# Two stages of normalised residual blocks: another order of the 26 products of a group, and set places in it for the next unit's preparation

## The chip, the cores and the metric

The kernel runs on one core of a Trainium2 chip. The core has a matrix engine (PE, whose weight loads the profile lists as PEld), three engines that work on vectors (DVE, ACT and POOL), and a queue on SyncE (SP) from which this kernel issues its DMAs, in order. The metric is the time of one execution on the device in microseconds (us); a version is given by the median of its runs.

## The reference

The input x is 2 × 2048 × 1024 in float32. Two blocks with a modulation computed from c follow each other: attention over the channels of a normalised x (a score matrix per position), and then, with nearly all of the work, a feed-forward network with 1024 inputs, 2752 hidden values and a SiLU gate:

```python
    mod = (_silu(L0_c) @ L0_wmod).reshape(L0_c.shape[0], 6, 1, -1)
    ...
    h = _layernorm(x, axis=-1) * (1 + ca) + sa
    x = x + ga * _L0_attn_ref(h)
    h = _layernorm(x, axis=-1) * (1 + cb) + sb
    x = x + gb * _L0_ffn_ref(h, L0_ffn_W_gate, L0_ffn_W_up, L0_ffn_W_down)
```

```python
        up = jnp.einsum('td,fd->tf', xf, W_up)
        gate = jax.nn.silu(jnp.einsum('td,fd->tf', xf, W_gate))
        h = gate * up
        y = jnp.einsum('tf,df->td', h, W_down)
```

## The kernel before

**Units.** The tokens are cut into 8 units of 256 tokens in each of the two batch entries. A unit has a *gate and up* part (hidden values, left in H) and a *down* part. All large products are made from float16 pairs: an operand is split into a high and a low half (`split`: L241 on ACT makes the high half, L245 on DVE the low one), and three of the four partial products are summed in float32.

**Gate and up.** Two tiles of 128 hidden values with their gate and up weights are a pair; there are 10 pairs of f-tiles, an extra tile (the 21st, number NP) and a left-over of 64 values. A pair can be computed *as is* (`gu_as_is`, 4 weight tiles with 48 matmuls of 128x256 each), or two pairs together as a *group* (`gu_group`): a fast matrix multiplication with 26 products where the plain way has 32. A product is 12 matmuls (L1110); the left operands (sums of weight blocks) are made once by `build` (after `G_LEFT`) and kept in DRAM as dq, the right operands (sums of blocks of the normalised x) once per unit by `right_gu` (after `G_RIGHT`). `G_STEPS` lists the 26 products in order: right operand, accumulator (six, on the PSUM tags X, Y, Z with two banks each), whether the accumulator is started anew, and the reads after it. A read is a copy to SBUF on ACT (`c`, L1114), an addition or subtraction on DVE (`+`, `-`, `r`, L1124), a SiLU on ACT (`s`, L1116) or the product of gate and up on DVE (`h`, L1120). `G_ROWS` says which block of the weights and tokens is which.

Unit 0 computes all pairs plainly and unit 1 as is. Units 2 to 7 run 3, 4, 5, 5, 5 and 5 groups, then what pairs are not in groups. Units 1, 2 and 3 build the left operands (3, 1 and 1 groups) beside their as-is pairs, with 2, 2 and 4 steps of `build` at each tick. After the pairs come the maximum for the scale of H (`close_scale`, L1156; it ends in L211, sA), tile NP as is, the right operand of down's first step (`right_dn(0)`, three L241 and three L245), and the left-over (`gu_left_over`, 48 matmuls at L1135 into pl; L1142 and L1143 on ACT and L1145 on DVE read pl).

**Down.** Seven products of a fast 2 × 2 scheme (`DN_STEPS`), 120 matmuls each (L1266, accumulators dX, dY, dZ); `right_dn(si + 1)` is issued in step si; then the left-over's share (L1294, pB), the results and their stores (L1303).

**Preparation of the next unit.** `prep(u + 1)` is a generator with 43 pieces: loads of x (L793) and of the statistics, 8 pieces that apply the first normalisation, 16 that add the attention's result, the mean (on POOL, L812), 8 that form and square the deviations (L831, L836, L837), the variance, its reciprocal root (L229 on ACT, L232 to L235 on DVE) and 8 that scale and shift (each with two L847 on DVE and two L849 on ACT). A part is run by `tick` during gate and up:

```python
                if u == 1 or taken % 4 == 0:
                    run_gen(side)
```

The rest runs in down, five pieces in each of its first three steps and what is left in the fourth. From the fourth step on, and beside pB, `right_gu` makes the right operands of the next unit.

**Weights.** `Feed` (L581) loads the weight tiles from DRAM in the order of use: a tile of a group holds two products (512 KB); four tiles are ahead, in a pool of 5 buffers, which one holds until its last matmul is done.

**Order.** In unit 0 the order of the instructions is as written. From unit 1 on a scheduler orders the instructions of each engine, so the text above gives only the order in which they are handed to it; `tick` ties its pieces behind the latest reads of DVE and ACT.

Of the kernel before, what the change touches and what calls it, by code (L numbers as in the profile page):

```python
# [45 lines left out]

G_STEPS = (
    (2, 4, True, (('c', 0),)),
    (10, 2, True, (('c', 1),)),
    (12, 3, True, (('c', 2),)),  # L50
    (17, 4, False, (('+', 1, 1),)),
    (3, 3, False, (('c', 3),)),
    (25, 1, True, (('+', 3, 3),)),
    (6, 4, False, (('c', 4),)),
    (0, 1, False, (('+', 2, 2),)),
    (8, 3, False, (('-', 1, 1), ('-', 4, 5),)),
    (16, 4, False, ()),
    (9, 0, True, (('-', 1, 1), ('s', 1),)),
    (7, 5, True, (('+', 4, 4),)),
    (20, 4, False, (('-', 3, 3), ('h', 3, 1, 0, 0),)),  # L60
    (1, 3, False, (('-', 4, 4),)),
    (14, 0, False, (('-', 0, 0),)),
    (21, 4, True, (('c', 1),)),
    (23, 5, False, (('-', 1, 3),)),
    (13, 3, False, (('-', 1, 1),)),
    (22, 1, False, (('+', 5, 5), ('+', 3, 3),)),
    (4, 0, True, (('-', 1, 1),)),
    (11, 4, True, (('+', 0, 0), ('-', 5, 5),)),
    (24, 2, False, (('+', 5, 5), ('s', 5),)),
    (15, 3, False, (('-', 0, 0), ('-', 3, 3), ('s', 0), ('s', 3), ('h', 1, 3, 1, 1),)),  # L70
    (5, 5, False, ()),
    (18, 0, False, (('-', 4, 4), ('h', 4, 5, 1, 0),)),
    (19, 5, False, (('-', 2, 2), ('h', 2, 0, 0, 1),)),
)

G_LEFT = (
    ('e', 13, 1, 1), ('e', 12, 4, 1), ('e', 17, 10, 1), ('o', 't', 12, '-', 0), ('e', 15, 't', 1),
    ('o', 0, 0, '+', 1), ('o', 12, 12, '-', 0), ('o', 't', 0, '-', 10), ('e', 2, 't', 1), ('o', 't', 12, '+', 9),
    ('e', 11, 't', 1), ('o', 't', 2, '-', 0), ('e', 21, 't', 1), ('o', 16, 10, '+', 11), ('e', 10, 16, -1),
    ('o', 16, 9, '-', 16), ('o', 10, 10, '+', 12), ('o', 't', 10, '-', 8), ('e', 14, 't', 1), ('o', 8, 0, '-', 8),  # L80
    ('o', 't', 8, '-', 9), ('e', 9, 't', 1), ('o', 9, 9, '-', 13), ('e', 24, 9, -1), ('o', 9, 9, '+', 15),
    ('o', 't', 9, '-', 11), ('e', 6, 't', -1), ('o', 0, 4, '+', 0), ('e', 3, 0, 1), ('o', 't', 0, '-', 16),
    ('e', 8, 't', -1), ('o', 't', 5, '+', 0), ('e', 16, 't', -1), ('o', 15, 15, '+', 16), ('o', 16, 1, '-', 16),
    ('e', 1, 16, 1), ('o', 13, 13, '-', 15), ('o', 15, 15, '+', 12), ('o', 't', 3, '+', 13), ('e', 18, 't', -1),
    ('o', 't', 13, '-', 7), ('e', 20, 't', -1), ('o', 't', 13, '-', 2), ('e', 7, 't', 1), ('o', 3, 3, '+', 2),
    ('o', 't', 3, '-', 16), ('e', 4, 't', -1), ('o', 7, 6, '+', 7), ('e', 25, 7, 1), ('o', 2, 2, '-', 14),
    ('e', 23, 2, -1), ('o', 6, 6, '+', 2), ('o', 't', 6, '-', 4), ('e', 5, 't', -1), ('o', 14, 14, '-', 7),
    ('o', 't', 15, '+', 14), ('e', 22, 't', 1), ('o', 14, 13, '-', 14), ('e', 0, 14, -1), ('o', 't', 5, '-', 14),
    ('e', 19, 't', -1),
# [1 line left out]
G_RIGHT = (  # L91
    ('e', 9, 0), ('e', 24, 1), ('e', 16, 2), ('e', 19, 3), ('e', 23, 4), ('e', 25, 5), ('e', 26, 6), ('e', 4, 7),
    ('o', 't', 7, '-', 4), ('e', 7, 't'), ('o', 't', 4, '-', 5), ('e', 21, 't'), ('o', 5, 5, '-', 7), ('e', 5, 5),
    ('o', 5, 1, '+', 5), ('e', 12, 5), ('o', 't', 1, '-', 0), ('e', 14, 't'), ('o', 8, 0, '-', 2), ('e', 8, 8),
    ('o', 't', 8, '-', 6), ('e', 10, 't'), ('o', 't', 8, '-', 5), ('e', 3, 't'), ('o', 5, 0, '-', 5), ('e', 2, 5),
    ('o', 't', 8, '-', 7), ('e', 1, 't'), ('o', 2, 6, '+', 2), ('o', 't', 6, '-', 7), ('e', 18, 't'),
    ('o', 6, 4, '-', 6), ('e', 6, 6), ('o', 't', 6, '+', 5), ('e', 17, 't'), ('o', 7, 3, '+', 7), ('e', 20, 7),
    ('o', 't', 4, '-', 7), ('e', 0, 't'), ('o', 't', 7, '-', 0), ('e', 11, 't'), ('o', 't', 2, '-', 7),
    ('e', 22, 't'), ('o', 't', 7, '-', 1), ('e', 15, 't'), ('o', 1, 1, '-', 3), ('o', 't', 1, '-', 8),
    ('e', 13, 't'),  # L100
)
G_OPERAND = (0, 1, 2, 3, 4, 5, 6, 7, 8, 9, 10, 11, 12, 13, 14, 15, 16, 17, 18, 19, 6, 5, 20, 21, 22, 23)
G_PLAIN = (9, 24, 16, 19, 23, 25, 26, 4)
G_ROWS = ((1, 1), (0, 1), (0, 0), (1, 0))

PARTS = ((0, 0), (0, 1), (1, 0))

# [2 lines left out]
def adaln_kernel(ctx, tc, x, xT, wgp, wg20, wgl, wd, wd20, wd21, wmod, cT, out, nunits=NU):  # L110
# [34 lines left out]
    def right_of(o):  # L145
        return homes[made.index(o)]
# [5 lines left out]
    def place(i):  # L152

        return mix[:, 3 * D + i * 2 * TU:3 * D + (i + 1) * 2 * TU]
# [62 lines left out]
    def sumsq(src, col):  # L217
        n = src.shape[-1] * (src.shape[-2] if src.ndim > 2 else 1)
        j = evp.tile([P, D], BF16, tag="junk", name="junk", bufs=1) if n <= D else mix[:, 4 * D:].bitcast(BF16)
        p = src.shape[0]  # L220
        jv = j[0:p, 0:n]
        if src.ndim > 2:
            jv = jv.rearrange("p (a b) -> p a b", a=src.shape[1])
        S.activation(jv, src, AF.Square, accum_out=col)  # L224
# [280 lines left out]
    def gu_src(p):  # L505
        return wgp[p] if p < NP else wg20
# [73 lines left out]
    class Feed:  # L580
# [16 lines left out]
        def take(self):  # L597
            w = self.w.pop(0)
            self.ahead()
            return w  # L600
# [17 lines left out]
    def build(groups):  # L618
# [13 lines left out]
        def load(q, i):  # L632
            pair, up = G_ROWS[i // 2]
            Q.dma_start(regions[i], gu_src(2 * q + pair)[:, 2 * up + i % 2])
# [103 lines left out]
    class LeftOver:  # L738

        r = hpf  # L740
# [350 lines left out]
    def run_gen(g):  # L1091
        return next(g, 0) != 0
# [4 lines left out]
    def gu_group(q, take, asq, tick):  # L1097

        inv = inv_q[:, q:q + 1]
        acc = [ps.tile([P, 2, TU], F32, tag="XYZ"[i % 3], name=f"p{i}") for i in range(6)]  # L1100
        e = [place(i).rearrange("p (f c) -> p f c", f=2) for i in range(5)]
        e.append(evp.tile([P, 2, TU], F32, tag="ev", name="e", bufs=3))
        for at, (r, a, first, reads) in enumerate(G_STEPS):
            if at % 2 == 0:
                w2 = take().rearrange("p (t h f k c) -> p t h f k c", t=2, h=2, f=2, k=2)
            w, right = w2[:, at % 2], right_of(G_OPERAND[r])
            for f in range(2):
                for k in range(2):
                    for j, (wa, ha) in enumerate(PARTS):
                        T.matmul(acc[a][:, f], w[:, wa, f, k], right[:, ha, k], start=first and f == 0 and k == 0 and j == 0,  # L1110
                                 stop=k == 1 and j == 2, skip_group_check=True)
            for x in reads:
                if x[0] == "c":
                    mark["act"] = S.copy(e[x[1]], acc[a])  # L1114
                elif x[0] == "s":
                    mark["act"] = S.activation(e[x[1]], e[x[1]], AF.Silu, scale=inv)  # L1116
                elif x[0] == "h":
                    _, u, s, pair, n = x
                    p = 2 * q + pair
                    mark["vec"] = V.scalar_tensor_tensor(H[:, 2 * p:2 * p + 2, n], e[u], inv, e[s], ALU.mult, ALU.mult)  # L1120
                else:
                    sign, src, dst = x
                    in0, in1 = (acc[a], e[src]) if sign == "r" else (e[src], acc[a])
                    mark["vec"] = V.tensor_tensor(e[dst], in0, in1, ALU.add if sign == "+" else ALU.subtract)  # L1124
            tick()
        for p in (2 * q, 2 * q + 1):
            sumsq(H[:, 2 * p:2 * p + 2].rearrange("p f n c -> p (f n c)"), asq[:, p:p + 1])

# [19 lines left out]
    def unit(u, side, nxt):  # L1148
# [33 lines left out]
        wd_last = prep_wd_last()  # L1182
        taken = 0

        def tick(*_):
            nonlocal taken
            taken += 1
            if "vec" not in mark:
                return

            with tc.issue_after(mark["vec"].ins), tc.issue_after(mark["act"].ins):
                if at_build is not None:
                    for _ in range(at_build[1]):
                        run_gen(at_build[0])
                if u == 1 or taken % 4 == 0:
                    run_gen(side)

        at_build = None
# [52 lines left out]
        for si, (a, i) in enumerate(DN_STEPS):  # L1251
# [7 lines left out]
            for mm in range(4):  # L1259
                h, j = mm // 2, mm % 2  # L1260
# [448 lines left out]
```

## Time and profile before

| | |
|---|---|
| median of 3 runs | 2580.16 us (2575.6 to 2580.39) |
| profiled execution | 2579.11 us, its span 2577.3 us, TensorE clock granted 0.993 |
| PE busy | 2502.1 us, 97% of the span |
| DVE, ACT, POOL busy | 1905.7, 1060.2 and 117.1 us |
| matmuls of groups (L1110) | 8424, 273 ns each, one started every 109 ns |
| weight tiles of groups (wg from dq) | 351, 512 KB, 4.2 us from issue to landing |

Busy times are what the engine's instructions cover; matmuls overlap each other, so that a matmul of 273 ns takes 109 ns of PE when the next is ready. "Idle before <- releaser" is the time in which the engine stood and what its next instruction waited for. The profiled execution's own time is 1.8 us over its span. The times of units, where pl's last matmul starts in gate and up, are 363.98, 698.36, 1010.58, 1311.08, 1602.90, 1892.65, 2182.87 and 2472.41 us from the start of the span.

### The profile page before, as it was taken

How to read it: one execution, taken by the hardware profiler on the slowest of the kernel's cores; microseconds unless marked ns; L12 is line 12 of the kernel's file. 1: busy time of each engine (PE TensorE's matmuls, PEld its weight loads, DVE VectorE, ACT ScalarE, POOL GpSimd, SP SyncE). 2: the span in 40 equal slices, each digit the busy share in tenths (PEclk: the TensorE clock that was granted, in tenths of full speed). 3: DMA queues.
4: the chain of work that ended last, by engine and by line, in shares of the span. 5: the costliest groups of instructions: out<-in, count | busy, mean ns of one | idle time of the engine just before them, and what ended most of it. 6: DMA issues, size and time to landing. Idle time of an engine off the chain costs nothing.

```text
span 2577.3 us, 50942 instructions
## 1 busy us (share of the span) xinstructions
PE 2502.1 (97%) x21399; PEld 2054.2 (80%) x21399; DVE 1905.7 (74%) x3275; ACT 1060.2 (41%) x1613; POOL 117.1 (5%) x68
## 2 busy tenths in 40 slices
PE   7899969999999999999999999999999999999999
PEld 2344438888888888888888888888888888888887
DVE  8778686488986676966898667966697767954473
ACT  7768764144641343523454224412353224412230
POOL 6210000000000000000000000000000000000000
PEclk9999989999999999999999999999999999999999
DMA  9988866688566665666766765666656755656654
GB/s 391 398 320 316 305 234 218 231 273 267 191 195 229 223 236 169 200 228 204 268 221 198 234 195 185 203 229 201 199 187 196 235 194 182 203 194 199 197 185 156
DMA packets 162325, 585.58 MB, mean 227 GB/s; under 512 B 17584, under 2 KB 17648, under 8 KB 162096
## 3 DMA queue, kind: packets, MB, share of 16 engines
q1 hardware_dynamic: 162096, 582.33, 66.6%
q8 instruction: 167, 2.74, 0.4%
q14 instruction: 62, 0.51, 0.1%
HBM read 490.48 MB, written 91.78 MB: 226 GB/s over the span
## 4 chain that ended last, share of the span: by engine, by line
PE 83%; DVE 6%; DMA 6%; ACT 2%; issue 2%; POOL 0%; SPq 0%; DVEq 0%; ACTq 0%; POOLq 0%
PE p L1110 31%; PE g L1077 14%; PE dY L1266 12%; PE dX L1266 8%; PE dZ L1266 8%; DMA wg<-dq 5%; PE g L1051 4%; PE pB L1294 3%; PE pl L1135 1%; DVE bst L362 1%; PE pm L277 1%; DVE hbt L245 1%; ACT wq L241 1%; DVE mix L245 0%; DMA H<-in_wgp_dram 0%
## 5 line engine op out<-in xcount | busy, mean ns | idle before, releaser
L1110 PEld LDWEIGHTS <-wg 128*128 128x128 f16 x8424 | 821.9, 98 | 124.3 <-DMA wg<-dq 23.1
L1266 PEld LDWEIGHTS <-wd 128*128 128x128 f16 x6720 | 659.4, 98 | 91.7 <-issue 13.8
L1110 PE MATMUL p<-hbt,wg 128*128 128x256 f16 x4536 | 533.6, 273 | 12.1 <-DMA wg<-dq 12.1
L1124 DVE TENSOR_TENSOR mix<-mix,p 128x512 f32<-128x512 f32 x486 | 324.8, 684 | 293.0 <-PE p L1110 214.9
L1110 PE MATMUL p<-rot,wg 128*128 128x256 f16 x3564 | 427.2, 273 | 3.2 <-DMA wg<-dq 3.2
L1077 PE MATMUL g<-hbt,wg 128*128 128x256 f16 x3744 | 411.2, 273 | 0.0
L1077 PEld LDWEIGHTS <-wg 128*128 128x128 f16 x3744 | 366.4, 98 | 43.0
L1266 PE MATMUL dY<-rot,wd 128*128 128x256 f16 x2880 | 318.6, 273 | 0.0
L241 ACT ACTIVATE rot<-H,sA 128x1024 f16<-128x1024 f32 x168 | 163.0, 1000 | 208.7 <-PE dY L1266 76.6
L1266 PE MATMUL dX<-rot,wd 128*128 128x256 f16 x1920 | 216.6, 275 | 12.7 <-issue 6.0
L1051 PE MATMUL g<-hbt,wq 128*128 128x512 f16 x1008 | 219.6, 379 | 8.4 <-DVE wq L245 3.6
L1114 ACT COPY mix<-p 128x512 f32<-128x512 f32 x162 | 92.1, 584 | 307.9 <-PE p L1110 307.0
L1266 PE MATMUL dZ<-rot,wd 128*128 128x256 f16 x1920 | 213.2, 273 | 0.0
L245 DVE SCALAR_TENSOR_TENSOR rot<-H,sA,rot 128x1024 f16<-128x1024 f32 x168 | 181.4, 1098 | 42.8 <-ACT rot L241 42.7
L1051 PEld LDWEIGHTS <-wq 128*128 128x128 f16 x1008 | 97.9, 98 | 131.5 <-issue 5.9
L224 ACT ACTIVATE junk<-H 128x1024 bf16<-128x1024 f32 (+1 forms) x102 | 101.1, 991 | 152.3 <-DVE H L1087 82.5
L1116 ACT ACTIVATE mix<-mix,inv_q 128x512 f32<-128x512 f32 x81 | 55.5, 716 | 139.6 <-DVE mix L1124 139.3
L1116 ACT ACTIVATE e<-e,inv_q 128x512 f32<-128x512 f32 x27 | 19.5, 722 | 176.3 <-DVE e L1124 176.3
L812 POOL PARTITION_ALL_REDUCE mean<-acc x6 | 19.4, 3234 | 1472.8 <-DVE acc L825 1147.0
L1120 DVE SCALAR_TENSOR_TENSOR H<-mix,inv_q 128x512 f32<-128x512 f32 x81 | 60.7, 750 | 19.7 <-ACT mix L1116 18.0
L1294 PE MATMUL pB<-mix 128*128 128x512 f16 x320 | 74.6, 379 | 0.0
L1247 DVE SCALAR_TENSOR_TENSOR big<-dY,cA,big 128x256 f32<-128x256 f32 x96 | 41.8, 476 | 43.0 <-PE dY L1266 43.0
(350 smaller groups left out, 2548.0 us busy)
## 6 DMA issues: line engine op xcount, KB each, us to landing
wg<-dq SPq DMA_DIRECT2D x351, 512.0 KB, 4.2
wd<-dwd SPq DMA_DIRECT2D x224, 640.0 KB, 4.0
dq<-mix SPq DMA_DIRECT2D x130, 256.0 KB, 3.3
wg<-dgu SPq DMA_DIRECT2D x64, 512.0 KB, 4.5
dgu<-wq SPq DMA_DIRECT2D x40, 512.0 KB, 7.2
dwd<-hbt SPq DMA_DIRECT2D x28, 640.0 KB, 3.4
out_dram<-big SPq DMA_DIRECT2D x30, 512.0 KB, 3.5
big<-in_xT_dram SPq DMA_DIRECT2D x28, 512.0 KB, 5.8
```

Source lines behind the costliest of these rows:

```text
L224: S.activation(jv, src, AF.Square, accum_out=col)
L241: mark["hi"] = S.activation(dst_hi, src, AF.Copy, scale=s)
L245: return V.scalar_tensor_tensor(dst_lo, src, s, dst_hi, ALU.mult, ALU.subtract)
L1051: T.matmul(pt[m, f].rearrange("p n c -> p (n c)"), w[:, wa, f, k], hb0[:, ha, 4 * kh + k], start=kh == 0 and k == 0 and j == 0, stop=kh == ...
L1077: T.matmul(pt[m, f][:, n], w[:, wa, f, k], plain_of(2 * kh + k // 2, n)[:, ha, k % 2], start=kh == 0 and k == 0 and j == 0 and n == 0, sto ...
L1110: T.matmul(acc[a][:, f], w[:, wa, f, k], right[:, ha, k], start=first and f == 0 and k == 0 and j == 0, stop=k == 1 and j == 2, skip_group ...
L1114: mark["act"] = S.copy(e[x[1]], acc[a])
L1116: mark["act"] = S.activation(e[x[1]], e[x[1]], AF.Silu, scale=inv)
L1120: mark["vec"] = V.scalar_tensor_tensor(H[:, 2 * p:2 * p + 2, n], e[u], inv, e[s], ALU.mult, ALU.mult)
L1124: mark["vec"] = V.tensor_tensor(e[dst], in0, in1, ALU.add if sign == "+" else ALU.subtract)
L1266: T.matmul(acc[a, h][:, j], w[:, k // 5, wa, k % 5], rot16[:, si % 2, ha, k], start=(a, h) not in seen, stop=k == KH - 1 and jj == 2, skip ...
L1294: T.matmul(pB, wt[:, k, wa, m, :], hp[:, k, ha, :], start=i == 0, stop=i == len(LAST) - 1)
```

## The change

The 26 products of a group come in another order and use other accumulators. The products, their number, and the number of DVE reads (22, and 4 products of gate and up) stay; the copies of accumulators to SBUF on ACT go from 6 to 8 for a group, and one read has its operands exchanged (`r`). The signs of some left operands change with it (`G_LEFT`), the right operands are made in another order (`G_RIGHT`), and the blocks get other places (`G_ROWS`).

`tick` now gets the place of the product in the group. In a group a piece of the preparation is run after the products 3, 7, 12, 17, 18, 22 and 25 (counted from 0; `G_PIECES`), where it was each fourth tick. At ticks of as-is tiles it is run each time in units 2 and later (each fourth time before), and in unit 1 at three ticks of four (each tick before). Counted over gate and up, this is 30 pieces where there were 41 in unit 1, 41 for 24 in unit 2, 40 for 29 in unit 3 and 39 for 33 in units 4 to 6; unit 7 prepares nothing.

```diff
--- before.py
+++ after.py
@@ -46,44 +46,44 @@
 
 G_STEPS = (
     (2, 4, True, (('c', 0),)),
-    (10, 2, True, (('c', 1),)),
-    (12, 3, True, (('c', 2),)),
-    (17, 4, False, (('+', 1, 1),)),
-    (3, 3, False, (('c', 3),)),
-    (25, 1, True, (('+', 3, 3),)),
-    (6, 4, False, (('c', 4),)),
-    (0, 1, False, (('+', 2, 2),)),
-    (8, 3, False, (('-', 1, 1), ('-', 4, 5),)),
+    (12, 2, True, (('c', 1),)),
+    (7, 3, True, (('c', 2),)),
+    (9, 5, True, (('c', 3),)),
+    (3, 2, False, (('c', 4),)),
+    (17, 4, False, (('+', 3, 3),)),
+    (25, 0, True, (('+', 4, 4),)),
+    (10, 1, True, (('+', 3, 3),)),
+    (6, 4, False, (('c', 5), ('+', 2, 2),)),
+    (14, 5, False, (('+', 0, 0),)),
+    (8, 2, False, (('-', 3, 3), ('-', 5, 5), ('s', 3),)),
+    (0, 0, False, (('+', 1, 1),)),
     (16, 4, False, ()),
-    (9, 0, True, (('-', 1, 1), ('s', 1),)),
-    (7, 5, True, (('+', 4, 4),)),
-    (20, 4, False, (('-', 3, 3), ('h', 3, 1, 0, 0),)),
-    (1, 3, False, (('-', 4, 4),)),
-    (14, 0, False, (('-', 0, 0),)),
-    (21, 4, True, (('c', 1),)),
-    (23, 5, False, (('-', 1, 3),)),
-    (13, 3, False, (('-', 1, 1),)),
-    (22, 1, False, (('+', 5, 5), ('+', 3, 3),)),
-    (4, 0, True, (('-', 1, 1),)),
-    (11, 4, True, (('+', 0, 0), ('-', 5, 5),)),
-    (24, 2, False, (('+', 5, 5), ('s', 5),)),
-    (15, 3, False, (('-', 0, 0), ('-', 3, 3), ('s', 0), ('s', 3), ('h', 1, 3, 1, 1),)),
-    (5, 5, False, ()),
-    (18, 0, False, (('-', 4, 4), ('h', 4, 5, 1, 0),)),
-    (19, 5, False, (('-', 2, 2), ('h', 2, 0, 0, 1),)),
+    (11, 5, True, (('+', 0, 0), ('-', 5, 5),)),
+    (20, 4, False, (('-', 4, 4), ('h', 4, 3, 1, 0),)),
+    (1, 2, False, (('-', 2, 2),)),
+    (24, 1, False, (('+', 5, 5),)),
+    (4, 5, True, (('c', 3),)),
+    (23, 3, False, (('c', 4),)),
+    (13, 2, False, (('-', 3, 3),)),
+    (18, 5, False, (('+', 2, 2), ('s', 2),)),
+    (21, 1, True, (('-', 3, 3), ('+', 4, 4), ('s', 3),)),
+    (5, 3, False, ()),
+    (15, 2, False, (('-', 0, 0), ('+', 4, 4), ('s', 0),)),
+    (19, 3, False, (('-', 1, 1), ('h', 1, 0, 1, 1),)),
+    (22, 0, False, (('+', 5, 5), ('r', 4, 4), ('h', 5, 2, 0, 0), ('h', 4, 3, 0, 1),)),
 )
 
 G_LEFT = (
...
-    ('e', 11, 't', 1), ('o', 't', 2, '-', 0), ('e', 21, 't', 1), ('o', 16, 10, '+', 11), ('e', 10, 16, -1),
+    ('e', 11, 't', 1), ('o', 't', 2, '-', 0), ('e', 21, 't', -1), ('o', 16, 10, '+', 11), ('e', 10, 16, -1),
...
-G_ROWS = ((1, 1), (0, 1), (0, 0), (1, 0))
+G_ROWS = ((0, 0), (1, 1), (1, 0), (0, 1))
+G_PIECES = (3, 7, 12, 17, 18, 22, 25)
 
 PARTS = ((0, 0), (0, 1), (1, 0))
 
@@ -1122,7 +1123,7 @@
                     sign, src, dst = x
                     in0, in1 = (acc[a], e[src]) if sign == "r" else (e[src], acc[a])
                     mark["vec"] = V.tensor_tensor(e[dst], in0, in1, ALU.add if sign == "+" else ALU.subtract)
-            tick()
+            tick(at)
         for p in (2 * q, 2 * q + 1):
             sumsq(H[:, 2 * p:2 * p + 2].rearrange("p f n c -> p (f n c)"), asq[:, p:p + 1])
 
@@ -1182,7 +1183,7 @@
         wd_last = prep_wd_last()
         taken = 0
 
-        def tick(*_):
+        def tick(at=None):
             nonlocal taken
             taken += 1
             if "vec" not in mark:
@@ -1192,7 +1193,7 @@
                 if at_build is not None:
                     for _ in range(at_build[1]):
                         run_gen(at_build[0])
-                if u == 1 or taken % 4 == 0:
+                if at in G_PIECES or at is None and (u > 1 or taken % 4):
                     run_gen(side)
 
         at_build = None
```

## The prediction

> **What bounds the kernel now.** I read the page first, then the waits of PE, the chain of waits inside one unit, and the timeline at the end of two units.
>
> ```profile
> PE 2502.1 (97%) x21399; PEld 2054.2 (80%) x21399; DVE 1905.7 (74%) x3275; ACT 1060.2 (41%) x1613; POOL 117.1 (5%) x68
> ```
>
> PE is busy for 97% of the span, and the change leaves its 21399 matmuls as many as they are. So the only stock to win from is the time in which PE stands, and the only way to lose is to make it stand elsewhere. The waits of PE (total us, times, longest):
>
> ```profile
> PE p L1110 <- DMA wg<-dq: 15.3, 28, 2.1
> PE dX L1266 <- issue: 6.0, 1, 6.0
> PE dX L1266 <- ACT rot L241: 4.5, 1, 4.5
> PE dX L1266 <- ACT up L1143: 1.5, 1, 1.5
> ```
>
> No wait of a group's products is on DVE or ACT; all 28 are on the weight tiles. The 6.0 lies in unit 0, which the change leaves alone; the 4.5 ends unit 1's gate and up, the 1.5 unit 2's. In the matmul rows, starts follow each other by 109 ns, and counted against that L1110 loses 21.0 us in 29 places. Three are at the start of a unit (0.72 at 818.5, 1.03 at 1124.6, 2.30 at 1423.4, together 4.05); the other 16.95 are inside groups: one before the fifth product of nearly every group, and a second, up to 1.56, in five groups. The chain of waits in unit 4's gate and up (start, us, what):
>
> ```profile
> 1418.27 7.53 DMA wg<-dq
> ...
> 1450.94 4.14 DMA wg<-dq
> ...
> 1485.47 4.27 DMA wg<-dq
> ```
>
> A tile lands some 4.2 us after its issue, the issue waits for a free buffer of the five, and products wait for the landing. The timeline of unit 1's end (start, us, engine, line, operation; in brackets the idle time before):
>
> ```profile
> 700.53 0.15 DVE L211 TENSOR_SCALAR sA<-p2c 128x1 int32<-128x1 int32 x1
> 700.57 0.68 ACT L1142 ACTIVATE mix<-pl,inv_f 64x512 f32<-64x512 f32 x1
> 701.26 0.68 ACT L1143 ACTIVATE up<-pl,inv_f 64x512 f32<-64x512 f32 x1
> 701.97 2.80 ACT L241 ACTIVATE rot<-H,sA 128x1024 f16<-128x1024 f32 x3
> 703.16 2.21 DVE L245 SCALAR_TENSOR_TENSOR rot<-H,sA,rot 128x1024 f16<-128x1024 f32 x2 [0.49 <-ACT rot L241]
> 703.17 0.58 PE L1266 MATMUL dX<-rot,wd 128*128 128x256 f16 x2 [4.54 <-ACT rot L241]
> 704.49 7.72 PE L1266 MATMUL dX<-rot,wd 128*128 128x256 f16 x51 [0.74 <-DVE rot L245]
> ```
>
> The left-over's last matmul started at 698.36. sA is late, then the work of the left-over (L1142, L1143) stands ahead of L241 on ACT. The first dX follows the start of L241 by 1.20, the third by 2.52. The first 20 matmuls after the pause also run at 213 ns. In all 7.8 us are lost. Unit 4 shows the good order:
>
> ```profile
> 1595.83 2.80 ACT L241 ACTIVATE rot<-H,sA 128x1024 f16<-128x1024 f32 x3 [2.12 <-DVE sA L211]
> ...
> 1605.10 0.68 ACT L1142 ACTIVATE mix<-pl,inv_f 64x512 f32<-64x512 f32 x1
> 1605.80 0.68 ACT L1143 ACTIVATE up<-pl,inv_f 64x512 f32<-64x512 f32 x1
> ```
>
> L241 is 7 us ahead of the left-over's last matmul (1602.90), and down begins at once (1603.01).
>
> **The change part by part.** (1) *Order of products, inside groups.* After unit 0 a scheduler orders every engine, so I read the order in which each kernel issues. In before it interleaves: products of one tile stand up to 8.3 products' time apart, that tile holds its buffer, and from the release of a buffer to the first need of the tile loaded into it there pass 3.93 us for 22 tiles and 1.31 for 5. Against a landing of 4.2 that makes the waits seen. In after nearly every tile (323 of 351) is done in two products of 1.31; the shortest time from release to need is 5.0, mostly some 10. So −16.95. The 54 added copies (L1114, 8 for 6 a group, 584 ns) give ACT 31.5 us more work; it is 41% busy, its last PSUM reader of a group still ends before the accumulator is wanted, and DVE has the same 22 reads and 4 products a group. Cost 0; without that cover each late read would cost up to its own 0.6 to 0.7 us in 27 groups, 16 to 18 in all. G_LEFT's signs and G_RIGHT's order change no count; the operands wanted first are made some 15 us ahead.
>
> (2) *Unit starts.* SP's queue is in order. In units 2 to 6 the third load of xT, which waits for an out store to land (3.5), now stands ahead of the fourth store, so the fifth tile's issue comes 0.3 to 0.4 later; but the new order needs that tile one product, 1.31, later. Of 4.05 I expect 0 to 2 to stay (most likely 1, in unit 4): −3.
>
> (3) *A quarter less preparation in unit 1* (30 pieces for 41). DVE and ACT reach the scale earlier; L241 now stands ahead of L1142 and L1143. sA falls at about pl's last matmul, so the first dX comes some 1.3 after, the third 1.3 later: 2.0 to 3.2 lost in place of 7.8, no 213 ns. −5.3 (−4.7 to −5.8). The eleven pieces go to down. There four L232 (3.3) now stand ahead of the third part of step 1's operand (L245); by the sum of the rows between it is still done 1.8 before its matmul, so 0, and up to 2 if the rows run longer.
>
> (4) *Unit 2.* dX's bank is no longer the left-over's, and the right operand is early: −1.6.
>
> (5) *The end of the preparation, units 4 to 6.* Before, 33 of 43 pieces came ahead of down; now 39, so r2 (L232 to L235) and nearly all scalings (L847 on DVE, L849 on ACT) fall between the last group and down. By the orders, DVE does four L232 (905 ns, 3.3 together), L233 to L235 and 13 L847 ahead of the maximum that makes sA, so sA comes 15.3 us after the last group against 15.62 for pl's last matmul. On ACT, 16 L849, L1142 and L1143 now stand ahead of L241. L1142 starts 0.3 after pl's last matmul; then 0.70, one L849 of 0.42, 0.69 and L241's first 1.20: dX starts 3.3 after pl, its third matmul another 1.3 behind. Less the 109 ns a start and the two matmuls, that is 4.3 a unit, 12.9 in all. What this wait stops is the whole of down. The clock may fall on top: 4.82 idle did it (20 × 104 ns = 2.1), 2.30 at 1423.4 did not; a wait of 3.2 lies between, nearer 2.30, but 1.2 follows soon. I take half of 0 to 6.3: +3.
>
> ```profile
> L849 ACT ACTIVATE big<-big,sbs 128x256 f32<-128x256 f32 x96 | 41.4, 496 | 3.9 <-DVE big L847 3.9
> L847 DVE SCALAR_TENSOR_TENSOR big<-big,b1s,r 128x256 f32<-128x256 f32 x96 | 38.9, 475 | 0.0
> ```
>
> The Trainium skill, TensorE: Matmul & The Clock Gate, Part 1, puts the gate at an idle window of about 3.4 us: by it the pause of unit 1 cools the array and the one of 2.30 does not, as the rows have it, and one of 3.2 would not either. By that page the sum would be 3.0 lower than mine.
>
> (6) *Unit 3.* There DVE also builds left operands, four a tick, and has no idle time: summing its instructions between two reads of gate gives 20.06 and the trace 19.99. Eleven more pieces make it 11 us later: sA at 62.2 to 62.9 after the last group (before: 50), pl's last matmul at 57.8, the first dX at 64.1, the third 1.3 on. 7.4, and 1.9 for the clock after so long a pause: +9.3 (7 to 12). If the scheduler's neighbours hide some of the scalings it is less, if they queue up more.
>
> (7) *Down of units 2 to 6* loses some preparation; PE had no wait there, so 0. Unit 7 prepares nothing: 0.
>
> Sum: −16.95 − 3 − 5.3 − 1.6 + 12.9 + 3 + 9.3 = −1.7. Against the profiled execution's 2579.1 (span 2577.3 and 1.8 around it) that is 2577.4. It stood 1.1 under the median of the runs, whose three lie within 4.8; I leave that in the range, and take 2577.
>
> **Rivals.** *A, the gain stays whole.* Pauses (5) and (6) are short because ACT's and DVE's orders let L241 slip through earlier, or the executed row times are shorter than my sums: −27 with 3 to 14 back, 2555 to 2566. For it: the gains rest on slack that is counted (5.0 against 4.2), the losses on instructions' places. Against it: places on ACT are fixed, and the left-over's end comes first there.
>
> *B, slower: the clock falls in units 3 to 6 each time, and unit 3's DVE falls further behind.* Three times 6.4, unit 3 at 12 to 14, against −26.9: +4 to +8, and with a unit start that keeps its 4 us up to +10: 2584 to 2589. It decides from an idle time of about 3 us that already halves the clock, and an sA of unit 3 later than 66.
>
> *C, the waits for weights only move.* If the order of issue lets the release slip (SP holds stores of dq and loads of xT ahead of wg), half of the 17 stays: +7, 2582 to 2588. For it: SP was what held unit 4's start for 7.53. Against it: in groups its idle is the rule.
>
> *D, a group's accumulators make PE wait* for L1114 or L1124: 27 × 0.3 = 8, 2580 to 2587. Against it: no such wait in before with DVE at 74%.
>
> **How the numbers follow.** The forecast's case 0.52, A 0.22, B 0.12, C 0.08, D 0.06. The forecast's own range is 2570 to 2584 by (2), the half of the clock and unit 3. The overall one leaves out the lower part of A and the upper part of B: 2560 to 2587. A measurement of this kernel can tell about 0.2%, 5.2 us, from no change: faster is under 2575.0, slower over 2585.3. All of A and a third of the forecast's case are faster: 0.40. Most of B, and half of C and D: 0.18. The rest is the same: 0.42.
>
> **What would show it.** After, L1110's waits on wg fall from 28 to a few; each is a step right. The waits of PE at dX should show L241 with four to five entries of 3 to 7 us, unit 1's under 2.5, and none on L1143. In units 4 to 6 the timeline should have L1142, L849, L1143, L241 in that order, and the 213 ns spacing of dX tells the clock. The forecast is wrong if L241 runs ahead of L1142 there (A), if L1110 waits on DVE (D), or if sA of unit 3 stands elsewhere than 62 us after the last group.

## The result, and the profile after

The changed kernel takes 2590.35 us (median of five runs, 2587.9 to 2591.46) against 2576.63 for the kernel before beside it (2574.67 to 2580.39): a ratio of 1.0043, interval 1.0032 to 1.0054. It is slower, by 0.4%, and the interval lies clear of 1. The profiled execution took 2590.82, its span is 2589.0, 11.7 more than the span before.

In the changed kernel's listing all lines from 106 on stand one higher (L1110 is L1111 there, L1266 is L1267). Busy time of each engine, from its page:

```profile
PE 2511.7 (97%) x21399; PEld 2061.0 (80%) x21399; DVE 1920.1 (74%) x3275; ACT 1095.3 (42%) x1667; POOL 115.2 (4%) x68
```

PE has the same 21399 matmuls and is busy 9.6 us longer. A part of that is stretches at half the rate, 213 ns apart for 109: behind the starts of down they cost 10.9 us, for 3.9 before, and the granted clock is 0.988 for 0.993. Its waits (total us, times, longest):

```profile
PE dX L1267 <- ACT rot L242: 18.9, 5, 9.0
PE dX L1267 <- DVE rot L246: 6.5, 5, 2.7
PE dX L1267 <- issue: 5.4, 1, 5.4
PE p L1111 <- DMA wg<-dq: 1.8, 5, 0.5
```

The waits of the groups' products for weights are nearly gone, 1.8 in 5 places for 15.3 in 28. In their place dX waits for its first operand five times: L242 and L246, the high and the low half. The chain of waits in unit 4's gate and up, where six stretches of 3.2 to 7.5 us were spent on wg, now has one, at the unit's start (the last line shows the products up to 1500; they run on without a wait to the end of the groups, at 1589.05):

```profile
1424.32 7.30 DMA wg<-dq
1431.63 0.05 issue
1431.67 68.40 PE p L1111 x625
```

The end of unit 1 in the timeline, with POOL:

```profile
700.88 0.14 DVE L212 TENSOR_SCALAR sA<-p2c 128x1 int32<-128x1 int32 x1
701.06 2.80 ACT L242 ACTIVATE rot<-H,sA 128x1024 f16<-128x1024 f32 x3 [1.27 <-DVE sA L212]
701.85 3.24 POOL L813 PARTITION_ALL_REDUCE var<-acc  x1 [38.33 <-DVE cA L1242]
702.24 3.86 DVE L246 SCALAR_TENSOR_TENSOR rot<-H,sA,rot 128x1024 f16<-128x1024 f32 x2 [0.41 <-ACT rot L242]
702.26 0.27 PE L1267 MATMUL dX<-rot,wd 128*128 128x256 f16 x1 [0.79 <-ACT rot L242]
...
705.23 14.76 PE L1267 MATMUL dX<-rot,wd 128*128 128x256 f16 x119 [2.70 <-DVE rot L246]
```

L242 comes right behind sA, as forecast. But the two L246 take 3.86 where they took 2.21 before, beside an all-reduce on POOL, and the second wait of dX is 2.70 for 0.74. And the end of unit 4:

```profile
1604.51 0.49 ACT L850 ACTIVATE big<-big,sbs 128x256 f32<-128x256 f32 x1
1604.73 0.15 DVE L212 TENSOR_SCALAR sA<-p2c 128x1 int32<-128x1 int32 x1
1605.03 0.68 ACT L1143 ACTIVATE mix<-pl,inv_f 64x512 f32<-64x512 f32 x1
1605.62 0.49 ACT L850 ACTIVATE big<-big,sbs 128x256 f32<-128x256 f32 x1
1606.12 0.68 ACT L1144 ACTIVATE up<-pl,inv_f 64x512 f32<-64x512 f32 x1
1606.83 2.80 ACT L242 ACTIVATE rot<-H,sA 128x1024 f16<-128x1024 f32 x3
1608.03 0.38 PE L1267 MATMUL dX<-rot,wd 128*128 128x256 f16 x2 [3.04 <-ACT rot L242]
1609.35 2.86 PE L1267 MATMUL dX<-rot,wd 128*128 128x256 f16 x14 [0.94 <-DVE rot L246]
```

This is the order L1143, L850, L1144, L242 that the prediction wrote down. pl's last matmul started at 1604.72, and sA was there at the same time. In unit 3 sA comes later still; pl's last matmul started there at 1304.94:

```profile
1312.87 0.15 DVE L212 TENSOR_SCALAR sA<-p2c 128x1 int32<-128x1 int32 x1
1313.06 2.80 ACT L242 ACTIVATE rot<-H,sA 128x1024 f16<-128x1024 f32 x3 [0.19 <-DVE sA L212]
1314.26 0.37 PE L1267 MATMUL dX<-rot,wd 128*128 128x256 f16 x1 [9.04 <-ACT rot L242]
```

The change of the span by places, each the sum of what PE's matmul starts lie over 109 ns apart (gaps of over 0.02 us), with the prediction's terms:

| place | before | after | difference | predicted |
|---|---|---|---|---|
| products inside groups | 15.8 | 0.1 | −15.7 | −16.95 |
| starts of units | 4.05 | 2.6 | −1.5 | −3 |
| left-over to down, unit 1 | 7.8 | 5.4 | −2.4 | −5.3 |
| the same, unit 2 | 1.6 | 0 | −1.6 | −1.6 |
| the same, unit 3 | 0 | 12.3 | +12.3 | +9.3 |
| the same, units 4 to 6 | 0 | 17.9 | +17.9 | +15.9 |
| unit 0 (pl's last matmul at 363.98 and 366.87) | | | +2.9 | 0 |
| sum | | | +11.9 | −1.7 |

The span grew by 11.7; the 0.2 between lies in gaps too small to be listed. The prediction's 16.95 was read too high: in the profile before, the starts of L1110 lie 19.9 us over 109 ns apart in 28 places, not 21.0 in 29, so that only 15.8 could be won inside groups.

Unit 0 issues the same instructions in the same order in both kernels. In all profiles of this study its last pl matmul lies between 363.98 and 368.52, and 363.98 is the profile of before: this 2.9 is the spread between executions, not the change.

### The profile page after: what moved, and what is told of

The parts are those of the page before. It is cut to its first block, busy times and chain, and to the rows that moved or that the text cites. A ratio compares the mean times of both kernels' runs of the same rounds, so it can differ in the third digit from the quotient of the medians.

```text
span 2589.0 us, 51078 instructions
## 1 busy us (share of the span) xinstructions
PE 2511.7 (97%) x21399; PEld 2061.0 (80%) x21399; DVE 1920.1 (74%) x3275; ACT 1095.3 (42%) x1667; POOL 115.2 (4%) x68
## 3 DMA queue, kind: packets, MB, share of 16 engines
q8 instruction: 167, 2.74, 0.4%
## 4 chain that ended last, share of the span: by engine, by line
PE 83%; DVE 6%; DMA 4%; ACT 3%; issue 3%; POOL 0%; SPq 0%; DVEq 0%; ACTq 0%; POOLq 0%
PE p L1111 34%; PE g L1078 13%; PE dY L1267 12%; PE dX L1267 9%; PE dZ L1267 8%; PE g L1052 2%; PE pB L1295 2%; DMA wg<-dq 1%; PE pl L1136 1%; DMA H<-in_wgp_dram 1%; DVE mix L246 1%; DMA mix<-in_wmod_dram 1%; PE pm L278 1%; DVE hbt L246 1%; ACT wq L242 1%
## 5 line engine op out<-in xcount | busy, mean ns | idle before, releaser
L1111 PEld LDWEIGHTS <-wg 128*128 128x128 f16 x8424 | 823.8, 98 | 105.0 <-DMA wg<-dq 3.4
L1267 PEld LDWEIGHTS <-wd 128*128 128x128 f16 x6720 | 662.6, 99 | 114.9 <-issue 33.1
L1111 PE MATMUL p<-hbt,wg 128*128 128x256 f16 x4536 | 534.8, 273 | 1.8 <-DMA wg<-dq 1.8
L1125 DVE TENSOR_TENSOR mix<-mix,p 128x512 f32<-128x512 f32 x459 | 307.2, 685 | 216.6 <-PE p L1111 146.4
L1111 PE MATMUL p<-rot,wg 128*128 128x256 f16 x3564 | 428.4, 273 | 0.0
L1267 PE MATMUL dY<-rot,wd 128*128 128x256 f16 x2880 | 318.6, 273 | 0.0
L242 ACT ACTIVATE rot<-H,sA 128x1024 f16<-128x1024 f32 x168 | 163.2, 1001 | 234.7 <-PE dY L1267 104.7
L1267 PE MATMUL dX<-rot,wd 128*128 128x256 f16 x1920 | 224.5, 281 | 30.8 <-ACT rot L242 18.9
L1115 ACT COPY mix<-p 128x512 f32<-128x512 f32 x189 | 109.6, 583 | 337.4 <-PE p L1111 239.4
L246 DVE SCALAR_TENSOR_TENSOR rot<-H,sA,rot 128x1024 f16<-128x1024 f32 x168 | 184.1, 1107 | 71.7 <-ACT rot L242 71.7
L1267 PE MATMUL dZ<-rot,wd 128*128 128x256 f16 x1920 | 212.9, 273 | 0.0
L1117 ACT ACTIVATE mix<-mix,inv_q 128x512 f32<-128x512 f32 x108 | 78.0, 722 | 186.3 <-DVE mix L1125 186.3
L1125 DVE TENSOR_TENSOR e<-e,p 128x512 f32<-128x512 f32 x108 | 73.6, 681 | 12.4 <-PE p L1111 12.4
L822 DVE SCALAR_TENSOR_TENSOR o<-big,alpha,o 128x256 f32<-128x256 f32 x96 | 44.3, 480 | 33.7 <-ACT o L821 33.6
```

What stands on the lines that cost most here:

```text
L242: mark["hi"] = S.activation(dst_hi, src, AF.Copy, scale=s)
L246: return V.scalar_tensor_tensor(dst_lo, src, s, dst_hi, ALU.mult, ALU.subtract)
L822: V.scalar_tensor_tensor(o[:, n], z[:, q, 1], alpha[:, n, 1, q:q + 1], o[:, n], ALU.mult, ALU.add)
L1267: T.matmul(acc[a, h][:, j], w[:, k // 5, wa, k % 5], rot16[:, si % 2, ha, k], start=(a, h) not in seen, stop=k == KH - 1 and jj == 2, skip ...
```

## The experiments

**Each half of the change alone.** First, the new order of products with the old rule for the pieces:

```diff
-                if at in G_PIECES or at is None and (u > 1 or taken % 4):
+                if u == 1 or taken % 4 == 0:
```

> The changed kernel with the old rule for the pieces (every tick in unit 1, every fourth later): the order of products alone. Theory (the order only frees weight buffers, the end of the preparation makes the pauses at down's start): PE's waits on wg in groups stay at some 2 us (17 less than before), unit 1 loses its 7.8 us again, units 3 to 6 lose nothing at the start of down, so some 17 to 19 us less than before, ratio 0.993. Rival (the new order itself ends its DVE and ACT work later and so makes sA late): the pauses of 3.2 us at down's start in units 4 to 6 stay, with 213 ns behind them, and the ratio is 1.000 or more.

Measured: 2561.6 us, ratio 0.9938 (0.9926 to 0.995). PE's waits at dX and in groups:

```profile
PE dX L1267 <- issue: 5.8, 1, 5.8
PE dX L1267 <- ACT rot L242: 4.4, 1, 4.4
PE dX L1267 <- ACT up L1144: 1.5, 1, 1.5
PE p L1111 <- DMA wg<-dq: 1.0, 1, 1.0
```

The waits for weights are gone but for 1.0, unit 1 loses its 7.8 and unit 2 its 1.6 as before, and units 3 to 6 lose nothing. The order of products is a pure gain; the rival falls.

Then the other half, the kernel before with the new places for the pieces (the rule above the other way round, with `tick(at)` and `G_PIECES`):

> The kernel before with the new places for the pieces, its own order of products. Theory: PE waits on wg as before (some 15 us in 25 to 30 places); unit 3 pauses for some 9 us before down. In units 4 to 6 ACT here has L241 ahead of the left-over's reads, so the pause is what sA's lateness alone makes, 1 to 1.5 us and another 1.2, without 213 ns or with little of it: 2 to 2.5 a unit. Unit 1 some 5.6 as in the changed kernel. Sum: -2 -1.6 +12 +7, ratio 1.005 to 1.007. Rival (late sA is the whole cost, ACT's order nothing): pauses of 3.2 and 1.1 and the cold clock in units 4 to 6 as in the changed kernel, +18, ratio 1.010.

Measured: 2593.05 us, ratio 1.0062 (1.0049 to 1.0074).

```profile
PE dX L1267 <- ACT rot L242: 14.2, 5, 8.4
PE p L1111 <- DMA wg<-dq: 10.7, 20, 1.3
PE dX L1267 <- DVE rot L246: 6.8, 5, 2.7
```

Unit 3 loses 11.1. In units 4 to 6 pl's last matmul is followed by pauses of 1.85 and 1.21, in one of the three units with the cold clock (matmuls 213 ns apart) behind them: 3.1, 4.4 and 3.1 lost, where the changed kernel loses 6.0 each. Weights are still waited for, somewhat less than before. So the pieces are the loss, and the halves don't simply add up: multiplied, the two ratios give 1.0000, the whole change gives 1.0043. 7.4 us of that difference lie in units 4 to 6; there ACT has L242 ahead of the left-over's reads here, and behind them in the changed kernel. The next run isolates this place.

**The left-over's reads on ACT.** In the changed kernel the two reads of pl were tied behind down's first operand:

```diff
-        S.activation(sl[0:FT], pl[0:FT], AF.Silu, scale=inv[0:FT])
-        S.activation(up[0:FT], pl[FT:P], AF.Copy, scale=inv[FT:P])
+        with ExitStack() as behind:
+            if u:
+                behind.enter_context(tc.issue_after(mark["hi", 0].ins))
+            S.activation(sl[0:FT], pl[0:FT], AF.Silu, scale=inv[0:FT])
+            S.activation(up[0:FT], pl[FT:P], AF.Copy, scale=inv[FT:P])
```

> The changed kernel with the left-over's two reads on ACT (L1143, L1144 there) put behind the three L242 of down's first operand, in all units. Theory (in units 4 to 6 L242 waited behind L1144, which waits for pl): the first dX comes 1.2 after sA's successor L242, about 1.3 after pl's last matmul for 3.2, the next wait of 1.1 stays, and the clock stays up: 2.4 lost for 6.0 in each of three units, so 11 less than the changed kernel, ratio to before 1.001. Units 1 and 3, where L242 already stands ahead, stay at some 5.6 and 12.3. Rival (sA is late, so order on ACT doesn't matter): the pauses stay within 0.3 us and the ratio is 1.004 to 1.005.

Measured: 2582.16 us, ratio 1.0017 (1.0008 to 1.0025). Unit 4's end in the timeline (L1146 and L1147 are the reads here):

```profile
1606.52 0.15 DVE L212 TENSOR_SCALAR sA<-p2c 128x1 int32<-128x1 int32 x1
1607.09 2.79 ACT L242 ACTIVATE rot<-H,sA 128x1024 f16<-128x1024 f32 x3
1608.28 0.27 PE L1270 MATMUL dX<-rot,wd 128*128 128x256 f16 x1 [1.50 <-ACT rot L242]
1609.59 3.65 PE L1270 MATMUL dX<-rot,wd 128*128 128x256 f16 x32 [1.05 <-DVE rot L246]
1609.78 0.67 ACT L1146 ACTIVATE mix<-pl,inv_f 64x512 f32<-64x512 f32 x1
```

sA is as late as in the changed kernel (it stands at pl's last matmul, 1606.50), but L242 starts 0.6 later and not 2.1. The pause is 1.66 for 3.20. By the ratios some 7 us less than the changed kernel, of which 6.3 lie in units 4 to 6 (2.9, 4.2 and 4.5 lost). The first part of the theory held. "The clock stays up" didn't: it fell in two of the three units, 3.0 us. Unit 1 stayed at 5.5. Unit 3 kept its pauses of 9.2 and 1.2, with a longer cold stretch behind them: 13.0 lost for 12.3.

**What lies before sA.** The pieces that are handed to the scheduler in down's steps aren't kept there by anything: it draws them ahead where the engine is free. Here they are tied behind down's first operand:

```diff
                 if si < READY:
-                    for _ in range(5):
-                        run_gen(side)
+                    with tc.issue_after(mark["lo", 0].ins), tc.issue_after(mark["hi", 0].ins):
+                        for _ in range(5):
+                            run_gen(side)
```

> The changed kernel; only the pieces that are left for down's first three steps are tied behind down's first operand (last L242 and L246), so that the scheduler can't draw them ahead of it. Theory (pieces drawn ahead delay sA and the operand): in units 4 to 6 eight scalings less stand ahead of sA, it comes 3.1 earlier, and L242 stands ahead of L1143: no pause there, 18 less. Unit 3 has six scalings less ahead of sA: 9 to 10 lost for 12.3. In unit 1 the all-reduce of the variance on POOL starts behind the operand, so the L246 that took 2.93 us beside it takes 1.2 to 1.3, and 3 to 4 less are lost with the clock. In all 23 to 25 less than the changed kernel, ratio to before 0.995 to 0.996. Rival (what counts is only the pieces that the ticks run): no change beyond 3 us, ratio 1.004.

Measured: 2563.38 us, ratio 0.9948 (0.9935 to 0.9962): this tie alone turns the loss into a gain. Unit 4:

```profile
1592.32 0.15 DVE L212 TENSOR_SCALAR sA<-p2c 128x1 int32<-128x1 int32 x1
1592.89 2.78 ACT L242 ACTIVATE rot<-H,sA 128x1024 f16<-128x1024 f32 x3
1595.59 6.60 PE L1267 MATMUL dX<-rot,wd 128*128 128x256 f16 x59
1595.79 0.68 ACT L1143 ACTIVATE mix<-pl,inv_f 64x512 f32<-64x512 f32 x1
```

sA is 3.2 ahead of pl's last matmul (1595.48) and PE doesn't pause. Unit 3 loses 9.9 for 12.3, unit 1 1.0 for 5.4, near what was expected. What unit 3 still loses comes of the pieces that the ticks themselves run beside the build: the two versions at the end, which run fewer there, lose 0 and 1.4.

**The all-reduce.** To tell whether POOL is what stretched L246, the sum over partitions was taken out of the preparation:

```diff
-            G.partition_all_reduce(t, acc, P, bass_isa.ReduceOp.add)
-            S.activation(t, t, AF.Copy, scale=1.0 / D)
+            S.activation(t, acc, AF.Copy, scale=1.0 / D)
```

> The changed kernel without the sum over the partitions in mean and variance of the next unit's preparation (POOL's all-reduce is left out, ACT scales the partition's own sums; the normalisation is not the reference's). Theory (DVE operations that read two operands from SBUF stand while POOL's all-reduce runs): in unit 1 the L246 of 2.93 us takes 1.2 to 1.3, the second pause at dX is 1.2 for 2.86 and the clock stays up, 5.4 lost become 2.2; unit 3's sA is 2 earlier, 12.1 become 10. Together 5 less, ratio to before 1.002 to 1.003. Rival (the 2.93 has another cause, a wait that the record hides): the pause of 2.86 stays, and the ratio 1.004 to 1.005.

Measured: 2587.87 us, ratio 1.0016 (1.0007 to 1.0026). The end of unit 1:

```profile
701.17 2.21 DVE L246 SCALAR_TENSOR_TENSOR rot<-H,sA,rot 128x1024 f16<-128x1024 f32 x2 [0.41 <-ACT rot L242]
701.19 0.27 PE L1266 MATMUL dX<-rot,wd 128*128 128x256 f16 x1 [0.79 <-ACT rot L242]
702.51 9.69 PE L1266 MATMUL dX<-rot,wd 128*128 128x256 f16 x72 [1.05 <-DVE rot L246]
```

The two L246 are back at 2.21, the second pause is 1.21 for 2.86, and in unit 3 sA (L212, at 1308.04) comes 64.3 us after the last group for 65.7. That part is shown. The clock still fell in unit 1 (16 matmuls at 213 ns), which the expectation had not, and in units 4 to 6 the cold stretches were longer this time (2.3 to 2.9 us for 1.67). The colder clock there takes back in this profile, with 2.8, nearly all that the two places gave (1.6 in unit 1, 1.5 in unit 3). By the medians this kernel is 2.5 us under the changed one, by the ratios some 7, because the kernel before beside it took 2582.77 here and 2576.63 there. So the verdict on the all-reduce rests on the timeline and not on the ratio.

**Why the old order waited for weights.** The prediction said that tiles are held because the products of different tiles are interleaved. Tying each matmul of a group behind the last, in the old list's order, takes the interleaving away and nothing else:

```diff
+                        with ExitStack() as behind:
+                            if "mm" in mark:
+                                behind.enter_context(tc.issue_after(mark["mm"].ins))
-                        T.matmul(acc[a][:, f], w[:, wa, f, k], right[:, ha, k], start=first and f == 0 and k == 0 and j == 0,
-                                 stop=k == 1 and j == 2, skip_group_check=True)
+                            mark["mm"] = T.matmul(acc[a][:, f], w[:, wa, f, k], right[:, ha, k],
+                                                  start=first and f == 0 and k == 0 and j == 0,
+                                                  stop=k == 1 and j == 2, skip_group_check=True)
```

> The kernel before with the matmuls of its groups tied in the order of its list, so that tiles are used one after the other and given back after two products. Theory (the waits for wg come of tiles held across other products): they go, from 14 to 20 us to under 4; the accumulators may make PE wait for DVE or ACT where the scheduler avoided it, up to 0.3 us a group, 8 in all. Ratio 0.993 to 0.998. Rival (the waits come of SP's queue, whichever way tiles are held): 12 us or more on wg stay, ratio 0.999 to 1.003.

Measured: 2577.05 us beside 2582.77, ratio 0.9975 (0.9961 to 0.9988). The groups' products have one line left among PE's waits, and none for wg:

```profile
PE p L1113 <- ACT mix L1118: 11.1, 25, 0.9
```

The waits for weights went, so they came of held tiles. But PE now waits up to 0.9 us in 25 places for the copy on ACT that gives an accumulator back (L1118 here is L1114 before). The gaps between the groups' products are 15.2 for 19.9. So the interleaved order was free of this wait, and had the other. What the new list brings is that it runs with next to none of either.

**Together.** Two versions that keep the gains. The first has the new order, three ticks of four in unit 1, each fourth tick from unit 2 on, and the pieces of down tied as above:

```diff
-                if at in G_PIECES or at is None and (u > 1 or taken % 4):
+                if (taken % 4 == 0) == (u > 1):
```

> The new order of products and the quarter less in unit 1, every fourth tick as before in units 2 and later, and the pieces left for down tied behind down's first operand. Theory: the gains add up: e1's 2561.6 less unit 1's 7.8 for 1.0, and up to 1.6 if unit 2's dX has a free bank; no pause before down in units 3 to 6. 2553 to 2556, ratio 0.990 to 0.992. Rival (pieces that come behind the first operand make the operand of the second step late): pauses of 1 to 2 us at the second step in five units, 2559 to 2564.

Measured: 2557.11 us beside 2582.77, ratio 0.9895 (0.9881 to 0.991). The only losses left at down's start from unit 1 on are 0.97 in unit 1 and 1.64 in unit 2; no second step pauses. The second, with the same tie and the same ticks in unit 1, has pieces in groups alone from unit 2 on:

```diff
-                if at in G_PIECES or at is None and (u > 1 or taken % 4):
+                if at in G_PIECES or at is None and u == 1 and taken % 4:
```

> As e4, and from unit 2 on the pieces run in groups alone (7 a group: 21, 28, 35, 35, 35 of 43), none at as-is ticks. Theory: unit 3 has 12 pieces less beside the build, sA comes before pl's end and its 9.9 us go: 2552 to 2556, ratio 0.990 to 0.992, as e5. Rival (in units 4 to 6 sixteen scalings now stand behind the first operand, 6 us on DVE ahead of the second operand's parts): the second step of down starts up to 2 us late in three units, 2557 to 2561.

Measured: 2558.37 us, ratio 0.9901 (0.9886 to 0.9916), the same within the intervals. Unit 3 loses 1.4, unit 1 1.0 and unit 2 nothing, and no second step of down pauses. The rival of both, scalings in the way of the second operand, didn't show. Both medians lie a little over the expected 2553 to 2556. The ratios, 0.9895 and 0.9901 for an expected 0.990 to 0.992, flatter them: the kernel before beside them was 5 us slower than beside the first four experiments. Against the order alone the first is 4.5 us better by the medians, 5.5 by the spans of the profiles and 11 by the ratios.

## Why the prediction was wrong

It gave 2577 with a range to 2587 and called no change the likeliest; it was 2590.35, and rival B, the slower one, came nearest. Of its two marks the clock did fall in units 3 to 6 each time; unit 3's scale came 65.7 us after the last group, just short of the 66 that it named. The median lies 1.4 over B's 2589.

The working had the mechanisms right. (1), the order inside groups, gave 15.7, all but 0.1 of what was there, where the misread 16.95 stood (shown by the order alone and by the old list in its own order). (4) gave its 1.6. In (5) the wait itself is right to a tenth: pauses of 3.20 and 1.10 in each of three units, 12.9 in all, as summed; both causes, the order on ACT and the late sA, are shown, each by the run that takes it away. In (7) nothing was lost in down. Without unit 0 the parts make +9.0 for −1.7. Of these 10.7, the order inside groups makes 1.2, and four terms that were too kind the rest:

- The clock in (5). The prediction took half of the possible cost, because 3.2 lay nearer to 2.30, which hadn't cooled the array, than to 4.82, which had. All three units cooled, 1.67 each: 5.0 for 3. The prediction saw that a pause of 1.2 follows soon, and gave it too little: the two matmuls between 3.20 and 1.10 of idle time didn't keep the clock up. The rule of the page TensorE: Matmul & The Clock Gate of the Trainium skill (Part 1), an idle window of some 3.4 us, was read as one unbroken pause, and by that reading 3.2 would not have cooled it at all. The measurement decides against that reading: the clock fell in all three units, and behind pauses of 0.96 and 1.21 too.
- Unit 1 in (3): 5.4 stayed for 2.0 to 3.2. L246 was priced at its mean of 1.28, and took 2.93 beside POOL's all-reduce; the pause of 2.86 then also cooled the array, 1.6 more. The step that failed is "the third 1.3 later ... no 213 ns".
- Unit 3 in (6): 12.3 for 9.3. The clock cost the 1.9 foreseen; sA was later than summed, 65.7 after the last group for 62.2 to 62.9. In the timeline an L246 beside POOL's all-reduce takes 2.0 longer, and with the all-reduce left out sA came at 64.3, 1.4 sooner. The rest, 1.4 to 2.1, was not sought.
- The starts of units in (2): 2.6 stayed for 1. Units 5 and 6, which had no gap before, have one of 0.5 to 0.6 at this place now. No run took this apart.

The second and third could have been read in the profile before. There POOL's all-reduce in unit 1 had also stretched an L245 to 2.73 us, at 668, where nobody waited for it. In the changed kernel's profile, unit 3:

```profile
1275.41 0.75 DVE L246 SCALAR_TENSOR_TENSOR mix<-rot,s_q,mix 128x512 f16<-128x512 f32 x1
...
1277.59 3.53 POOL L813 PARTITION_ALL_REDUCE var<-acc  x1 [43.12 <-DVE acc L838]
1277.94 2.74 DVE L246 SCALAR_TENSOR_TENSOR mix<-rot,s_q,mix 128x512 f16<-128x512 f32 x1
```

The same operation takes 0.75 alone and 2.74 beside POOL.

## What to carry to other kernels

Work that is put off to a later stage in the program's text isn't put off in the schedule: if the scheduler finds a free engine, it draws the work ahead, in front of the operand on which the next stage starts; tie it behind that operand. A change that moves work can hold a gain and a loss of the same size, and measuring the halves separately shows which to keep: here 0.9938 and 1.0062, and 0.9895 with the order and the lighter unit 1 kept and the rest tied. And where a mean duration prices an instruction on the path, look at its longest one first, and at what ran beside it.

## What the runs showed of the hardware

**DVE stands beside POOL's all-reduce.** Operations of DVE with two operands from SBUF took 2.62 to 2.93 us where they take 0.68 to 1.28 alone, when they began within 0.5 us after the start of a PARTITION_ALL_REDUCE of 3.2 to 3.6 us. Subtracting their own time, they went on some 2.0 to 2.4 us after POOL's start, so before its end. L1125, which reads one operand from PSUM, kept its 0.68 beside the same operation in units 4 to 6. The Trainium skill, SBUF — State Buffer, section "Who interferes with whom", says that a DVE instruction with two SBUF inputs contends with a GpSimd instruction that reads SBUF, and that one with at most one SBUF input, outside the 2-port perf modes, doesn't. For these operations the runs agree, only that the block ended before the record of POOL's instruction did. But a TENSOR_SCALAR with one tensor and a scalar for each partition, 0.23 alone, stood too: in the profile before, cB (L1243) took 2.20 at 1036.48, 0.07 behind POOL's start, and cA (L1241) 0.90 in each of units 4 to 6. No run shows in which mode it ran. And it goes the other way round: with the pieces of down tied, two L246 were running when the all-reduce of unit 1 began (723.33), and its record lasted 5.06, for 3.24 without the tie.

**Two short pauses cool the array**, that is, the matmuls behind them run at half the rate. What the clock did after pauses at the start of down, in all profiles, from unit 1 on (a cold stretch is 13 to 28 matmuls at 213 ns):

| pauses, us | units seen | clock fell |
|---|---|---|
| one, 0.97 | 3 | 0 |
| one, 1.4 to 1.64 | 5 | 0 |
| one, 2.30 (a group's start, before) | 1 | 0 |
| 0.96 and 1.21, one matmul between | 1 | 1 |
| 1.66 and 1.21, one matmul between | 3 | 2 |
| 1.85 and 1.21, one matmul between | 3 | 1 |
| 0.95 and 2.86, one matmul between | 3 | 3 |
| 3.20 and 1.04 to 1.10, two matmuls between | 6 | 6 |
| 4.6 to 4.7 and 1.04 | 3 | 3 |
| 6.8 to 9.2 and 1.21 | 5 | 5 |

A sum of 2.2 to 3.1 us of idle time within at most 3.3, broken by a matmul, sometimes halved the clock, and 3.8 and more did it each time. Why the same pauses did it in one unit and not in the next stays open; that a pause's place in time decides is a guess that no run here tested. From unit 1 on no pause over 2.30 came without a second one behind it, so these runs don't show what 3.2 alone would have done.
